# Mamba layer: four engines in the written order, steps of the prologue and epilogue three or four states apart, additions to the sum five states back

## The chip, the cores and the metric

The kernel runs on one core of one Trainium2 chip. The metric is the device time of one execution in microseconds (us). The program computes a stack of eight layers on an activation of 8 sequences x 256 tokens x 128 channels in fp32; the change lies in the seventh of them, `l3_attn`, a bidirectional Mamba layer.

## The reference, cut to what matters

```python
def _mamba(x, ...):                       # E = 256 channels, N = 64 states, R = 8, K = 4
    xp, z = jnp.split(x @ W_in.T, 2, axis=-1)
    xc = _silu(depthwise_conv(xp, conv_w) + conv_b)
    dt_lo, Bm, Cm = split(xc @ W_xp.T, (R, N, N))
    dt = softplus(dt_lo @ W_dt.T + dt_b)
    A = -jnp.exp(A_log)                   # E x N
    def step(h, inp):                     # over 256 tokens
        dA = jnp.exp(dtt[:, :, None] * A)
        h = dA * h + (dtt * xt)[:, :, None] * Bt[:, None, :]
        y = jnp.einsum('ben,bn->be', h, Ct)
        return (h, y)
    y = ys + xc * Dp
    return (y * _silu(z)) @ W_out.T

# the layer: x + norm(ref(norm(x))), where ref is
xn = _layernorm(x, ln1_w, ln1_b)
x1 = _mamba(xn, m1...)
x2 = flip(_mamba(flip(xn), m2...))
return _layernorm(x1 + x2, ln2_w, ln2_b) + xn
```

## The kernel before, in words

The sequences go two at a time: four groups g, and in each the forward Mamba (m = 0) and the backward one (m = 1), which makes eight units u of 64 states each, 512 states in all. A state is one of the N = 64 columns of A, and its work for a whole unit is done at once: a tile of 128 channels x (2 sequences x 2 channel halves x 256 tokens), 128x1024 fp32.

One pass i of the main loop handles several states in different phases:

- `start(i)`: SP fetches C of the state over all partitions (`Cs`, five buffers); ACT computes `dA` = exp(dt*A) in two instructions (L2053, three buffers), and for even states four scaled copies `sT` (L2050).
- `inputs(i-1)`: PE writes the input term of the state into PSUM, `ps_h`, by eight transposes of `sT` (L2068, even states) or by 32 small products with `dB` (L2066, odd states). POOL makes `dB` for two odd states at a time (L2040, `pre`). `ps_h` shares three PSUM buffers (tag "b") with every `ps_a` of the prologue and the epilogue.
- `scan(i-1)`: DVE runs the recurrence over all 1024 columns (L2074) into `h` (three buffers). Then h is multiplied with C into `hc` (L2076, four buffers): on POOL, and in every eighth state on DVE, where the scan works in place in PSUM.
- `add(i-4)`: PE adds `hc` to the sum of the unit, `ps_y`, by eight transposes (L2086). There is one buffer of `ps_y`.

Between these lie the steps of two generators, one step a pass: `behind` is the epilogue of the unit that has just ended, and `ahead` is the prologue of the next one, begun in pass n = 6 of a unit. A `yield` ends a step. The prologue normalises x (m = 0 only; `norm_steps` twice, and ln1 on POOL, L1916 and L1917), transposes it (L1924 or L1926, copy L1928), convolves (L1937, L1939), projects (L1944, L1946), applies Silu (L1948), makes B, C and dt (L1953, L1956, L1959 to L1970) and dtx (POOL, L1973; PE L1983, ACT L1985). The epilogue copies `ps_y` (ACT, L1992), transposes it back (PE, L1997), adds D*xc (DVE, L2001, two instructions), multiplies with silu(z) (POOL, L2003) and projects (PE, L2009); after m = 1 it also adds x1 and x2 (DVE, L2022), normalises (`norm_steps`, twice) with three POOL operations between (L2024, L2026, L2028) and one at the end (L2033).

`norm_steps` is DVE statistics (L227, L228), two small POOL operations for the inverse root (L230, L231), a small DVE operation on their result (L234), and four ACT instructions (L237).

The first six layers run under `as_written`, which chains the instructions of PE, DVE, ACT and POOL in the order in which the program issues them. The Mamba layer does not: there the compiler's list scheduler decides the order on each engine from the dependencies, and it moves steps against each other. SP's queue is under the scheduler in both.

Of the kernel before, what the change touches and what calls it, by code (L numbers as in the profile page):

```python
# [8 lines left out]
F32 = mybir.dt.float32  # L9
# [3 lines left out]
ALU = mybir.AluOpType  # L13
# [159 lines left out]
class Ctx:  # L173
# [45 lines left out]

    def norm_steps(self, dst, src, n):  # L220

        nc = self.nc
        st = self.small.tile([P, n, 6], F32, name="ln_st")
        mv = self.small.tile([P, n, 2], F32, name="ln_mv")
        rs = self.small.tile([P, n], F32, name="ln_rs")
        for i in range(n):
            nc.vector.bn_stats(out=st[:, i, :], in_=src[:, i, :])  # L227
            nc.vector.bn_aggr(out=mv[:, i, :], in_=st[:, i, :])  # L228
        yield
        nc.gpsimd.tensor_scalar(rs, mv[:, :, 1], EPS, None, ALU.add)  # L230
        nc.gpsimd.tensor_tensor(rs, rs, self.mhalf.to_broadcast([P, n]), ALU.pow)  # L231
        for i in range(4):
            yield
        nc.vector.scalar_tensor_tensor(mv[:, :, 0], mv[:, :, 0], -1.0, rs, ALU.mult, ALU.mult)  # L234
        yield
        for i in range(n):
            nc.scalar.activation(dst[:, i, :], src[:, i, :], AF.Identity, bias=mv[:, i, 0:1], scale=rs[:, i:i + 1])  # L237
        yield
# [1609 lines left out]
def l3_attn(k):  # L1848
# [17 lines left out]
    with ExitStack() as es:  # L1866
# [10 lines left out]
        for m, w in enumerate(k.l3a):  # L1877


            w["wk"] = s1.tile([P, 4, 256], F32, name="wk", bufs=2)  # L1880
            cv = s2.tile([P, 4, 256], F32, name="cv", tag="sp_u")
            nc.sync.dma_start(out=cv, in_=k.I[f"l3a_m{m + 1}_conv"].partition_broadcast(P))
            nc.vector.tensor_tensor(w["wk"], cv, over(w["win"][:, 0:256], 4, 1), ALU.mult)
            w["A"] = s1.tile([P, 2, N], F32, name="A", bufs=2)
            nc.scalar.activation(w["A"], w["alog"], AF.Exp)
            nc.vector.tensor_scalar(w["A"], w["A"], 1e-20, -1.0, ALU.max, ALU.mult)
        xTs, CLs = [], []
        for j in range(2):
# [20 lines left out]
        def prologue(u, o):  # L1909
            g, m = divmod(u, 2)  # L1910
            w = k.l3a[m]
            if m == 0:
                xs = xns[g] = s2.tile([P, 4, D], F32, name="xn")
                yield from k.norm_steps(xs, k.x[:, 4 * g:4 * g + 4, :], 4)
                yield from k.norm_steps(xs, xs, 4)
                nc.gpsimd.tensor_tensor(xs, xs, over(k.l3a_ln[:, 0, :], 4, 1), ALU.mult)  # L1916
                nc.gpsimd.tensor_tensor(xs, xs, over(k.l3a_ln[:, 1, :], 4, 1), ALU.add)  # L1917
                yield
            xT, CL = xTs[u % 2], CLs[u % 2]
            ps = pb()  # L1920
            for j in range(4):
                d = slice(j * P, (j + 1) * P)
                if m == 0:
                    nc.tensor.transpose(ps[:, 0, d], xns[g][:, j, :], k.ident)  # L1924
                else:
                    nc.tensor.matmul(ps[:, 0, d], xns[g][:, j ^ 1, :], k.flip, start=True, stop=True)  # L1926
            yield
            nc.scalar.copy(xT[:, :, 3:3 + L], by_seq(ps[:, 0, :]))  # L1928
# [4 lines left out]
            for ec in range(2):  # L1933
                for b in range(2):
                    ps = pb()
                    for tap in range(4):
                        nc.tensor.matmul(ps[:, 0, 0:L], w["wk"][:, tap, ec * P:(ec + 1) * P], xT[:, b, tap:tap + L], start=tap == 0, stop=tap == 3)  # L1937
                    yield
                    nc.scalar.activation(xc[:, ec, b * L:(b + 1) * L], ps[:, 0, 0:L], AF.Identity, bias=w["cols"][:, ec, 0:1])  # L1939
                    yield  # L1940
                    yield
            for ec in range(2):
                ps = pb()
                nc.tensor.matmul(ps[:, 0, :], w["win"][:, 256 + ec * P:256 + (ec + 1) * P], xT[:, :, 3:3 + L], start=True, stop=True)  # L1944
                yield
                nc.scalar.copy(sz[:, ec, :], ps[:, 0, :])  # L1946
# [7 lines left out]
            for j in range(4):  # L1954
                for ec in range(2):
                    nc.tensor.matmul(ps[:, 1, j * 64:(j + 1) * 64], xc[:, ec, j * P:(j + 1) * P], w["wxp"][:, ec, 0:64], start=ec == 0, stop=ec == 1)  # L1956
            yield
            B = s2.tile([P, 4, N], F32, name="B")
            nc.scalar.copy(CL[0:72, :], ps[0:72, 0, :])  # L1959
# [8 lines left out]
            dt = s2.tile([P, 2, U], F32, name="dt")  # L1968
            yield
            nc.scalar.activation(dt, ps, AF.Softplus)  # L1970
            yield
# [4 lines left out]
            yield  # L1976
            yield
            dtxT = s2.tile([P, 4, 2, P], F32, name="dtxT")
            ps = pb()
            for j in range(4):  # L1980
                for ec in range(2):
                    n = 2 * j + ec
                    nc.tensor.transpose(ps[:, n // 4, n % 4 * P:(n % 4 + 1) * P], dtx[:, ec, j * P:(j + 1) * P], k.ident)  # L1983
            yield
            nc.scalar.copy(dtxT.rearrange("p (a j) e c -> p a (j e c)", a=2), ps)  # L1985
            o.update(xc=xc, sz=sz, cd=cd, dt=dt, dtxT=dtxT, dtxTt=turned("dtxTt", dtxT), B=B, Bt=Bt)

        def epilogue(u, o):
# [3 lines left out]
            nc.scalar.copy(yT.rearrange("p j e c -> p (j e c)"), o["py"].rearrange("p j e c -> p (j e c)"))  # L1992
            yield
            py = pb()
            for ec in range(2):
                for j in range(4):
                    nc.tensor.transpose(py[:, ec, j * P:(j + 1) * P], yT[:, j, ec, :], k.ident)  # L1997
            yield
            t = s2.tile([P, 2, U], F32, name="t", tag="sp_u")
            for ec in range(2):  # L2000
                nc.vector.scalar_tensor_tensor(t[:, ec, :], o["xc"][:, ec, :], w["cols"][:, ec, 2:3], py[:, ec, :], ALU.mult, ALU.add)  # L2001
            yield
            nc.gpsimd.tensor_tensor(t, o["sz"], t, ALU.mult)  # L2003
            yield
            yield
            ps = pb()
            for j in range(4):
                for ec in range(2):
                    nc.tensor.matmul(ps[:, 0, j * D:(j + 1) * D], t[:, ec, j * P:(j + 1) * P], w["wout"][:, ec, :], start=ec == 0, stop=ec == 1)  # L2009
            xs = s2.tile([P, 4, D], F32, name=f"x1{m}")  # L2010
            yield
            nc.scalar.copy(xs.rearrange("p i d -> p (i d)"), ps[:, 0, :])
# [5 lines left out]
            for j in range(4):  # L2018
                nc.tensor.matmul(ps[:, 0, j * D:(j + 1) * D], k.flip, xs[:, j ^ 1, :], start=True, stop=True)
            yield  # L2020
            xs = x1s[g]
            nc.vector.tensor_tensor(xs, ps[:, 0, :].rearrange("p (i d) -> p i d", d=D), xs, ALU.add)  # L2022
            yield from k.norm_steps(xs, xs, 4)
            nc.gpsimd.tensor_tensor(xs, xs, over(k.l3a_ln[:, 2, :], 4, 1), ALU.mult)  # L2024
# [3 lines left out]
            nc.gpsimd.tensor_tensor(xs, xs, xns[g], ALU.add)  # L2028
            yield
            yn = s2.tile([P, 4, D], F32, name="yn")  # L2030
            yield from k.norm_steps(yn, xs, 4)
            to = k.x[:, 4 * g:4 * g + 4, :]
# [37 lines left out]
        def scan(st, n):  # L2070
            flat = "p b e t -> p (b e t)"
            on_v = n % ON_V == ON_V - 1
            h = st["in"] if on_v else s3.tile([P, 2, 2, L], F32, name="h")
            nc.vector.tensor_tensor_scan(h.rearrange(flat), st["dA"].rearrange(flat), st["in"].rearrange(flat), 0.0, ALU.mult, ALU.add)  # L2074
            st["hc"] = s1.tile([P, 2, 2, L], F32, name="hc", bufs=4)
            (nc.vector if on_v else nc.gpsimd).tensor_tensor(st["hc"], h, over(by_seq(st["C"]), 2, 2), ALU.mult)  # L2076

        def add(o, st, n):

            if n == 0:  # L2080
                o["py"] = psumy.tile([P, 4, 2, P], F32, name="ps_y")
            for b in range(2):
                for j in range(2):
                    for ec in range(2):
                        first = n == 0 and j == ec == 0
                        nc.tensor.matmul(  # L2086
                            o["py"][:, 2 * b + j, ec, :], st["hc"][:, b, ec, j * P:(j + 1) * P], k.ident,
                            start=first, stop=n == N - 1, is_transpose=True, skip_group_check=True,
                        )
# [7 lines left out]
        for n in range(3):  # L2097
            pre(made[0], n)
        for i in range(units * N + 4):
            u, n = divmod(i, N)  # L2100
# [12 lines left out]
            if 1 <= i <= units * N:  # L2113
                scan(sts[i - 1], c)
            if i >= 4:
                v, c = divmod(i - 4, N)
                add(made[v], sts.pop(i - 4), c)
                if c == N - 1:
# [56 lines left out]
def program(tc, I, out, layers):  # L2175
    nc = tc.nc
    with ExitStack() as es:
# [39 lines left out]
        for layer in (l3_attn, l3_ffn):  # L2217
            if layer in layers:
                layer(k)
        held[-1].__exit__(None, None, None)  # L2220
# [19 lines left out]
```

## Time and profile before

| | us |
|---|---|
| median of 3 runs | 4112.87 (4107.72 to 4126.58) |
| profiled execution, its own time | 4108.04 |
| its span, first to last instruction | 4106.3 |
| Mamba loop, first scan to last `hc` (2671 to 4023) | 1352 |
| in it: DVE busy / POOL busy / ACT busy / PE busy | 1229.4 / 1239.7 / 1192.5 / 1186.6 |
| granted TensorE clock in the loop | 0.98 |

In the rows of the profile a group of instructions stands with its line, engine, operation, tiles, count, busy time, mean duration in ns, and behind the bar the idle time of the engine just before it with what ended it. "Idle before" in the rows of a timeline stands in square brackets with the releaser. Busy time of two consecutive instructions can overlap a little, so the distance from start to start is used where it is known.

### The profile page before, as it was taken

The page shows a single profiled execution, that of the slowest core. Times are in us where ns is not written, and L with a number is a line of the kernel's source. Part 1 is how long each engine was busy: PE and PEld are TensorE (multiplying, and loading weights), DVE is VectorE, ACT ScalarE, POOL GpSimd, SP SyncE. Part 2 cuts the span into 40 slices and gives each one's busy share as a digit, 9 for nine tenths or more (in the row PEclk, how much of TensorE's full clock was granted, in tenths as well). Part 3 has the DMA queues.
Part 4 walks back from the last instruction along what each step waited for, and adds up shares of the span by engine and source line. Part 5 has one row for each costly group of instructions (what it writes and reads, how often), then busy time and mean ns, then how long its engine had stood idle before and what let it go on. Part 6 is the DMA issues. An engine that isn't in the chain of part 4 may idle for free. (4 is left out here: it accounts for less than half of the span.)

```text
span 4106.3 us, 125005 instructions
## 1 busy us (share of the span) xinstructions
PE 3556.8 (87%) x55183; PEld 2808.9 (68%) x55183; DVE 3015.5 (73%) x4210; ACT 2541.2 (62%) x4481; POOL 2651.4 (65%) x1991
## 2 busy tenths in 40 slices
PE   6899898988898888899998977698988988898886
PEld 4777787777777656565565554387777876877774
DVE  7667768767666666654477677289979988998995
ACT  4445455544445545565454443399979988898893
POOL 5666857856665554522133344389989988998993
PEclk8999999999999999999999998799999999999997
DMA  2000000000001000000000000033323333333430
GB/s 58 3 3 2 3 3 2 3 3 8 3 23 34 1 1 12 20 6 21 1 1 1 6 1 1 26 105 112 110 81 116 111 100 93 111 112 91 115 114 26
DMA packets 98677, 168.89 MB, mean 41 GB/s; under 512 B 16699, under 2 KB 26582, under 8 KB 98006
## 3 DMA queue, kind: packets, MB, share of 16 engines
q1 hardware_dynamic: 98134, 160.89, 13.2%
q8 instruction: 433, 7.09, 0.7%
q14 instruction: 110, 0.90, 0.1%
HBM read 153.51 MB, written 2.10 MB: 38 GB/s over the span
## 5 line engine op out<-in xcount | busy, mean ns | idle before, releaser
L2076 POOL TENSOR_TENSOR hc<-h,Cs 128x1024 f32<-128x1024 f32 x448 | 1050.1, 2373 | 97.8 <-DVE h L2074 85.8
L2074 DVE TENSOR_TENSOR_SCAN h<-dA,ps_h 128x1024 f32<-128x1024 f32 x448 | 989.1, 2267 | 88.9 <-PE ps_h L2068 54.0
L2053 ACT ACTIVATE dA<-dt,A 128x512 f32<-128x512 f32 x1024 | 684.4, 715 | 125.1 <-DVE h L2074 92.2
L2086 PE MATMUL ps_y<-w_c_ident,hc 128*128 128x128 f32 x4096 | 560.9, 281 | 116.1 <-POOL hc L2076 84.1
L2086 PEld LDWEIGHTS ps_y<-w_c_ident,hc 128*128 128x128 f32 x4096 | 453.0, 143 | 171.4 <-POOL hc L2076 156.0
L2050 ACT ACTIVATE sT<-dtxT,B 128x256 f32<-128x256 f32 x1024 | 449.8, 495 | 5.7 <-PE ps_h L2068 5.7
L590 DVE SCALAR_TENSOR_TENSOR acc<-ps,w_l0a_conv,acc 128x254 f32<-128x254 f32 (+2 forms) x768 | 310.3, 472 | 46.9 <-ACT acc L584 46.7
L2066 PE MATMUL ps_h<-dB,dtxTt 64*64 64x64 f32 x16384 | 301.8, 223 | 19.3 <-DVE h L2074 10.1
L2066 PEld LDWEIGHTS ps_h<-dB,dtxTt 64*64 64x64 f32 x16384 | 266.2, 136 | 72.9 <-issue 46.4
L2068 PE MATMUL ps_h<-w_c_ident,sT 128*128 128x128 f32 x2048 | 277.3, 280 | 19.5 <-DVE h L2074 16.9
L2068 PEld LDWEIGHTS ps_h<-w_c_ident,sT 128*128 128x128 f32 x2048 | 240.2, 145 | 31.6 <-DVE h L2074 23.9
L742 POOL TENSOR_TENSOR Ps<-M,w_c_levels 128x512 f32<-128x512 f32 x192 | 241.3, 1274 | 7.2 <-DVE M L716 6.2
L230 POOL TENSOR_SCALAR ln_rs<-ln_mv 128x4 f32<-128x4 f32 (+1 forms) x84 | 22.0, 263 | 336.8 <-DVE ln_mv L228 307.0
L359 ACT COPY XY<-ps 128x1024 f32<-128x1024 f32 (+1 forms) x116 | 108.6, 947 | 152.8 <-PE ps L807 140.5
L800 PE MATMUL ps<-Z,XY 64*64 64x64 f32 x4608 | 169.5, 224 | 21.8 <-DVE Z L784 14.5
L807 PE MATMUL ps<-XY,Z 64*64 64x64 f32 x5120 | 168.8, 222 | 3.5 <-issue 3.5
L800 PEld LDWEIGHTS ps<-Z,XY 64*64 64x64 f32 x4608 | 142.1, 135 | 42.2 <-DVE Z L784 19.3
L1633 ACT ACTIVATE e<-ps,nm 128x256 f32<-128x256 f32 x256 | 99.9, 481 | 96.8 <-DVE nm L1630 69.5
L781 PE MATMUL ps<-XY,Ps 64*64 64x64 f32 x5120 | 115.9, 226 | 48.4 <-issue 11.7
L2074 DVE TENSOR_TENSOR_SCAN ps_h<-dA,ps_h 128x1024 f32<-128x1024 f32 x64 | 145.6, 2275 | 14.9 <-PE ps_h L2066 14.6
L784 DVE TENSOR_TENSOR Z<-ps,w_c_ident 128x512 f32<-128x512 f32 x160 | 107.8, 686 | 60.1 <-PE ps L781 58.6
L807 PEld LDWEIGHTS ps<-XY,Z 64*64 64x64 f32 x5120 | 148.6, 136 | 4.2 <-issue 4.2
(452 smaller groups left out, 8559.8 us busy)
## 6 DMA issues: line engine op xcount, KB each, us to landing
Cs<-cd SPq DMA_DIRECT2D x512, 256.0 KB, 3.3
dtxTt<-dtxT SPq DMA_DIRECT2D x32, 128.0 KB, 4.0
wk<-in_l0a_w SPq DMA_DIRECT2D x8, 256.0 KB, 6.8
w_h<-in_l1f_h SPq DMA_DIRECT2D x4, 512.0 KB, 6.0
w_l2a<-in_l2a_w SPq DMA_DIRECT2D x3, 512.0 KB, 3.8
w_l0a_wg<-in_l0a_wg SPq DMA_DIRECT2D x1, 1024.0 KB
w_qk<-in_l0f_wqkv SPq DMA_DIRECT2D x2, 512.0 KB, 5.3
cv<-in_l3a_m_conv SPq DMA_DIRECT2D x2, 512.0 KB, 4.9
```

What stands on the lines that cost most here:

```text
L590: nc.vector.scalar_tensor_tensor(acc[:, n, s:L], p4[:, n, 0:L - s], conv[:, h2, 4 * j + n, 3 - s:4 - s], acc[:, n, s:L], ALU.mult, ALU.add,)
L742: nc.gpsimd.tensor_tensor(t, M[:, :, 0:64], over(k.l0a_levels[:, n, :], 8, 1), ALU.mult)
L781: nc.tensor.matmul(ps[to, a, at(j)], Ps[own, h, :], XY[own, t, at(i)], start=True, stop=True)
L800: nc.tensor.matmul(ps[own, a, at(j)], XY[rows, t, at(i)], Z[rows, za, at(zj)], start=True, stop=True)
L807: nc.tensor.matmul(ps[to, a, at(4 + j)], Z[rows, za, at(zj)], XY[rows, t, at(i)], start=True, stop=True)
L2050: nc.scalar.mul(st["s"][:, j], o["dtxT"][:, j], o["B"][:, j, n:n + 1])
L2053: nc.scalar.activation(dA[:, :, ec, :], by_seq(o["dt"][:, ec, :]), AF.Exp, scale=w["A"][:, ec, n:n + 1])
L2066: nc.tensor.matmul(ps[q, b, ec, j * 64:(j + 1) * 64], o["dtxTt"][rows, j, ec, q], dB[rows, j, :], start=True, stop=True)
L2068: nc.tensor.transpose(ps[:, j // 2, ec, j % 2 * P:(j % 2 + 1) * P], st["s"][:, j, ec, :], k.ident)
L2074: nc.vector.tensor_tensor_scan(h.rearrange(flat), st["dA"].rearrange(flat), st["in"].rearrange(flat), 0.0, ALU.mult, ALU.add)
L2076: (nc.vector if on_v else nc.gpsimd).tensor_tensor(st["hc"], h, over(by_seq(st["C"]), 2, 2), ALU.mult)
L2086: nc.tensor.matmul(o["py"][:, 2 * b + j, ec, :], st["hc"][:, b, ec, j * P:(j + 1) * P], k.ident, start=first, stop=n == N - 1, is_transpos ...
```

## The change

The Mamba layer now runs under `as_written` on PE, DVE, ACT and POOL. Its generators get more `yield`s, so that a step on one engine and the step that uses its result lie two to four passes apart where it was one. `add` works five states back rather than four, with five buffers of `hc`. `norm_steps` takes the number of passes before the DVE step and before the ACT step, and has a form in which one pass stands for two normalisations in a row (var*(1+EPS)+EPS*EPS under the root); the prologue's two become one. The D*xc term moves from DVE to PE: eight products of `xc` with a diagonal tile `D` open the sum `ps_y`, and the epilogue's two DVE instructions and its POOL multiplication become one DVE multiplication of `ps_a` with silu(z). Two diagonal tiles are made at the layer's start.

```diff
-    def norm_steps(self, dst, src, n):
+    def norm_steps(self, dst, src, n, twice=False, steps=(4, 1)):
...
-        nc.gpsimd.tensor_scalar(rs, mv[:, :, 1], EPS, None, ALU.add)
+        if twice:
+            nc.gpsimd.tensor_scalar(rs, mv[:, :, 1], 1.0 + EPS, EPS * EPS, ALU.mult, ALU.add)
+        else:
+            nc.gpsimd.tensor_scalar(rs, mv[:, :, 1], EPS, None, ALU.add)
         nc.gpsimd.tensor_tensor(rs, rs, self.mhalf.to_broadcast([P, n]), ALU.pow)
-        for i in range(4):
+        for i in range(steps[0]):
             yield
         nc.vector.scalar_tensor_tensor(mv[:, :, 0], mv[:, :, 0], -1.0, rs, ALU.mult, ALU.mult)
-        yield
+        for i in range(steps[1]):
+            yield
...
+            w["D"] = s1.tile([P, 2, P], F32, name="D", bufs=2)
+            for ec in range(2):
+                nc.vector.tensor_scalar(w["D"][:, ec, :], k.ident, w["cols"][:, ec, 2:3], None, ALU.mult)
...
-                yield from k.norm_steps(xs, k.x[:, 4 * g:4 * g + 4, :], 4)
-                yield from k.norm_steps(xs, xs, 4)
+                yield from k.norm_steps(xs, k.x[:, 4 * g:4 * g + 4, :], 4, True, (3, 3))
...
-                yield
+                for _ in range(4):
+                    yield
...
             yield
+            yield
             nc.scalar.copy(xT[:, :, 3:3 + L], by_seq(ps[:, 0, :]))
...
             t = s2.tile([P, 2, U], F32, name="t", tag="sp_u")
-            for ec in range(2):
-                nc.vector.scalar_tensor_tensor(t[:, ec, :], o["xc"][:, ec, :], w["cols"][:, ec, 2:3], py[:, ec, :], ALU.mult, ALU.add)
-            yield
-            nc.gpsimd.tensor_tensor(t, o["sz"], t, ALU.mult)
+            nc.vector.tensor_tensor(t, py, o["sz"], ALU.mult)
+            yield
...
-            yield from k.norm_steps(xs, xs, 4)
+            yield from k.norm_steps(xs, xs, 4, steps=(3, 3))
...
-            st["hc"] = s1.tile([P, 2, 2, L], F32, name="hc", bufs=4)
+            st["hc"] = s1.tile([P, 2, 2, L], F32, name="hc", bufs=5)
...
             if n == 0:
                 o["py"] = psumy.tile([P, 4, 2, P], F32, name="ps_y")
+                for j in range(4):
+                    for ec in range(2):
+                        nc.tensor.matmul(
+                            o["py"][:, j, ec, :], o["xc"][:, ec, j * P:(j + 1) * P], w["D"][:, ec, :],
+                            start=j % 2 == ec == 0, stop=False, skip_group_check=True,
+                        )
...
-        for i in range(units * N + 4):
+        for i in range(units * N + 5):
...
-            if i >= 4:
-                v, c = divmod(i - 4, N)
-                add(made[v], sts.pop(i - 4), c)
+            if i >= 5:
+                v, c = divmod(i - 5, N)
+                add(made[v], k.l3a[v % 2], sts.pop(i - 5), c)
...
-                layer(k)
+                with as_written(tc, COMPUTE if layer is l3_attn else ()):
+                    layer(k)
```

The same single `yield` is added after the PE step of the convolutions, of both projections, of B and C, of dt, of the transposed dtx, and in the epilogue after L1992, L1997, L2009 and L2019; two more are added after dtx.

## Prediction

> **What bounds the kernel now.** First the stage. The busy times in the Mamba loop (columns: stretch, its length, then busy us and instructions of PE, PE weight load, DVE, ACT and POOL, then the granted clock):
>
> ```profile
> 2671.00:4023.00 1352.00, 1186.64 (x23218) 1046.04 (x23218) 1229.42 (x683) 1192.50 (x2207) 1239.68 (x630) 0.98 0.36 105
> ```
>
> DVE and POOL each work some 91% of it. Neither can shrink much, so what an edit can win is the 1352 - 1229.4 = 122.6 us in which DVE stands still. The groups that make the load:
>
> ```profile
> L2076 POOL TENSOR_TENSOR hc<-h,Cs 128x1024 f32<-128x1024 f32 x448 | 1050.1, 2373 | 97.8 <-DVE h L2074 85.8
> L2074 DVE TENSOR_TENSOR_SCAN h<-dA,ps_h 128x1024 f32<-128x1024 f32 x448 | 989.1, 2267 | 88.9 <-PE ps_h L2068 54.0
> ```
>
> By the timeline seven scans in a row start 15.25 us before the next one (2.18 each), and a state on DVE takes 2.31 + 1.15 = 3.46. Eight states: 7 x 2.18 + 3.46 = 18.72 on DVE. Four `hc` in a row take 9.28 (2.32 each), a `dB` 1.02; POOL's eight are 7 x 2.32 + 2 x 1.02 = 18.28. So POOL gains only 0.44 per eight states: whatever else it gets, DVE soon waits for through the three buffers of `h`. Then DVE's waits in the loop (us, times, longest):
>
> ```profile
> DVE h L2074 <- PE ps_h L2068: 54.0, 17, 35.7
> DVE ln_mv L234 <- POOL ln_rs L231: 30.4, 10, 3.7
> DVE h L2074 <- PE ps_h L2066: 15.9, 15, 3.2
> DVE ps_h L2074 <- PE ps_h L2066: 14.6, 6, 3.4
> DVE ln_st L227 <- POOL x L2028: 13.3, 3, 4.5
> DVE t L2001 <- PE ps_a L1997: 8.3, 7, 1.9
> DVE h L2074 <- POOL hc L2076: 8.2, 9, 1.8
> ```
>
> Without the 35.7 before the first scan, and with four smaller rows (10.3), they make 119.3. The second and fifth rows, 43.7 us, are small normalisation steps that the scheduler put ahead of scans. The timeline shows one such place, third unit:
>
> ```profile
> 3027.78 2.37 POOL L2076 TENSOR_TENSOR hc<-h,Cs 128x1024 f32<-128x1024 f32 x1 [0.77 <-DVE h L2074]
> 3030.42 1.04 POOL L231 TENSOR_TENSOR ln_rs<-ln_rs,mhalf 128x4 f32<-128x4 f32 x1
> 3031.49 0.17 DVE L234 SCALAR_TENSOR_TENSOR ln_mv<-ln_mv,ln_rs 128x4 f32<-128x4 f32 x1 [3.06 <-POOL ln_rs L231]
> ...
> 3038.30 0.29 DVE L227 BATCH_NORM_STATS2 ln_st<-x 128x6 f32<-128x128 f32 x1 [4.44 <-POOL x L2028]
> ...
> 3040.84 1.97 PE L2068 MATMUL ps_h<-w_c_ident,sT 128*128 128x128 f32 x8 [4.93 <-DVE h L2074]
> ```
>
> DVE stands 3 us for a 0.17 us instruction whose input lies behind an `hc`; PE then runs dry and its eight transposes take 1.97 where they take 1.04 elsewhere. The PE rows of the waits come mostly from here (second unit):
>
> ```profile
> 2927.22 1.94 PE L1953 MATMUL ps_a<-xz,w_l3a_m_wxp 128*72 128x512 f32 x4 [0.39 <-ACT xz L1948]
> 2928.99 1.89 PE L1956 MATMUL ps_a<-w_l3a_m_wxp,xz 128*128 128x64 f32 x16
> 2930.82 1.16 PE L2066 MATMUL ps_h<-dB,dtxTt 64*64 64x64 f32 x64
> ...
> 2932.10 2.30 DVE L2074 TENSOR_TENSOR_SCAN ps_h<-dA,ps_h 128x1024 f32<-128x1024 f32 x1 [3.37 <-PE ps_h L2066]
> ```
>
> The B and C projection waits for Silu, holds PE for 3.6, and the next state's input stands behind it.
>
> **The change part by part, against the profiled execution (4108.04; span 4106.3).**
>
> *Normalisation waits.* In the new order L234 stands four passes behind the statistics and the second L227 two behind L2028, each pass a scan of 2.18. POOL is at most some 5.5 behind (2.37 for its own `hc`, up to 2.9 lag), plus 1.25 for L230 and L231: under four passes. The 43.7 goes. What is late next is POOL itself, below.
>
> *DVE's own work in the loop.* Seven pairs of L2001 at 1.41 become one multiplication from PSUM; nearest row L2076 on DVE, 1.22 (upper bound the pair): 7 x 0.19 = -1.3. Double norms: groups 2 and 3 lose 1.3 each, group 1, formerly done before the loop, brings 1.3. Together -2.6.
>
> *POOL's own work.* L2003 goes (7 x 2.37). There remain, outside the eights, in the loop: dtx 7 x 2.45 = 17.2, roots 9 x 1.27 = 11.4, L2024, L2026, L2028 and L2033 for three groups 15.2, L1916 and L1917 for three 7.6: 51.4. From this come off at most 64 x 0.44 = 28 of slack and 22 of DVE's own small work lying beside it. So 1 to 51 of DVE waits. Taken: 28, by places: dtx 15.8 (each 2.45 less 0.4, more where roots stand before it), L1916/L1917 3 x 1.6, the epilogue's four operations and roots 3 x 2.4.
>
> *PE at Silu and dt.* These steps keep one `yield` between Silu and L1953. Silu ends 4.5 after the scan that frees its pass's `dA`; PE 3.5 later; the input 1.1 more: 9.2, where a scan is due at 7.7 (pass 26, after a DVE state: wait 1.5, four times) or 6.5 (pass 38: 2.7, three times): 14.1. The dt product (1.7 before an input) costs 0.85 x 7 = 6. Sum 20; from 0, if the new lag hides it, to 34, as the three `ps_h` rows have now less the 14 that other steps may own.
>
> *PSUM buffers.* The extra yields hold a `ps_a` one pass longer. In the built program 152 of the 512 inputs wait for the scan two back (127 before), and six for the scan just before: passes 6 and 15 of units 2, 4, 6. Each of the six costs 1.04 to 1.16 and some 0.2: 1.25. Pass 12 waits for an ACT copy after a later `dA`: 0.7. In pass 6 of the four odd and three even units the eight transposes L1997 are late by 0.8 or 1.1. Sum 3 x 3.25 + 3 x 1.1 + 4 x 0.8 = 16. The trace has no such place; bounds 0 and 40, if each second `ps_a` pair behaves so.
>
> *D on PE.* 8 products a unit; L2009 has eight of them at 1.95, eight transposes (L2068) 1.04: 8 to 16 us on PE in all. They stand between an input and `add(0)`, wait for the copy L1992, and end 0.3 before the next input is due. On the path: nothing; without that cover up to 8 x 1.9 = 15.
>
> A rule bears on PE. The eight transposes of a state take 1.04 in the timeline, at a granted clock of 0.98; a pair of states needs 2 x 2.18 of DVE and some 3.9 of PE, so PE has room. The Trainium skill, "TensorE: Matmul & The Clock Gate", Part 4, says that transposes do not count as PE activity, that the clock does not rise to full for them, and gives some 275 ns each. By that estimate three groups of eight would hold PE 6.6 a pair and the layer would gain nothing. The row contradicts it.
>
> *Lag five.* `add` then asks for an `hc` one scan older: 2.2 more before POOL's lag stops PE. It is what makes the 28 a cost through `h` alone; SP's `Cs` (five buffers, landing 3.3) still has over 5 us.
>
> *Start.* In DVE's new order both `wk` (1.2 each, behind the fetch of `cv` that lands at about 2628), A and D stand ahead of the statistics of x, which had been done at 2618. Statistics end at 2633.1, roots, ACT and POOL to 2639.2, where L1924 started at 2633.9: +5.3, in spite of the norm saved. ACT loads Exp after four `sT`, +1.3. First scan +6.6, bounds 3 and 9; the wait before the second scan falls from 3.2 to 1.
>
> *Tail.* L2001 and L2003 (1.41 + 2.4) become 1.22: -2.5.
>
> Sum: waits 119.3 become 28 + 20 + 16 + 1 = 65, so -54; -2.6; +6.6; -2.5: -52.7. 4108.0 - 52.7 = 4055. The median stands 4.8 above the profiled execution: 4060.
>
> **Rivals.**
>
> *The waits nearly all go* (15%). If the longer lags let POOL catch up in the eights, the remaining waits are 1 + 20. Then -98 -2.6 + 6.6 - 2.5, so 4012 (4016 by the median). For it: POOL's load after, 1239.7 - 17.9 + 2.5 = 1224, is no more than DVE's 1227. Against: bursts of 2.45 meet a slack of 0.44.
>
> *No gain* (12%): POOL's 51 in full, PE's 34, PSUM's 30: 116 stay, and the start: -3.3 - 2.6 + 6.6 - 2.5, so 4106 (4111). For it: today's waits on POOL may only be shifted, since DVE has waited there anyway. Against: POOL stood still for 97.8 before `hc`, so it is not what is full.
>
> *Slower* (7%): the PSUM buffers become the bound. Some 100 `ps_a` are made in the loop, each held about two passes; if an input has to wait for the scan just before, it costs 1.25. At 42 such inputs the -52.7 is gone; at 100, 125 - 52.7 = +72: 4180. For it: three buffers for everything, each `ps_a` held longer. Against: six such waits in the built program. That an order is in fact not kept is no rival: the instruction lists of the changed program show the scans unbroken and L234 four scans late.
>
> **How the numbers follow.** Forecast 66%, rivals 15, 12 and 7. A measurement of this kernel can tell some 0.5% (20.6 us) from no change. The forecast's own bounds, POOL 28 less 20 or plus 15 and PE and PSUM about 12 either way, give 4030 to 4090; the range reaches halfway into the two neighbours, 4020 to 4098. Faster (under 4092): nearly all of the forecast and the first rival, 80%. Same 12, slower 8.
>
> **What would show it.** The waits of DVE: no row `ln_mv <- POOL ln_rs` and none on L2028 in the loop; a row of scans waiting for `hc` of 15 to 40 us in place of 8.2. The timeline: a gap of 1.5 to 3 at each L1953, 1.25 at passes 6 and 15 of units 2, 4 and 6. First scan at about 2678. Wrong: a DVE idle sum in the loop above 100, or waits on PSUM in every pass of a prologue.

## The result, and the profile after

The changed kernel takes 4075.9 us (median of 4 runs, 4074.5 to 4079.5); the kernel before took 4119.7 beside it. The ratio is 0.9904, with a 95% interval of 0.9879 to 0.9929: faster by about 1%. The profiled execution took 4076.06 with a span of 4074.1, so 32.2 us of span less than before. The forecast was 4060 (4055 for the profiled execution). The sign held; of the 53 us forecast 32 came between the two profiled executions and 44 between the medians. The terms of the sum were less good than the total.

The same stretch of the profile, with the columns of before (stretch, length, busy us and instructions of PE, weight load, DVE, ACT and POOL, then granted clock, DMA share and GB/s):

```profile
2675.00:3991.00 1316.00, 1180.78 (x23338) 1037.85 (x23333) 1238.21 (x667) 1166.77 (x2205) 1224.63 (x625) 1.00 0.37 108
```

The loop, from the first scan to the end of the last state's `hc` (DVE's; in the change POOL's last one ends 0.9 later), went from 1351.8 to 1315.3. DVE's idle time in it went from 122.4 to 77.1, but its busy time rose from 1229.4 to 1238.2: it had been forecast to fall. The two large groups of the page hardly moved, as they must:

```profile
L2094 POOL TENSOR_TENSOR hc<-h,Cs 128x1024 f32<-128x1024 f32 x448 | 1051.4, 2372 | 95.3 <-DVE h L2092 94.8
L2092 DVE TENSOR_TENSOR_SCAN h<-dA,ps_h 128x1024 f32<-128x1024 f32 x448 | 993.4, 2269 | 93.5 <-ACT dA L2071 44.6
```

DVE's waits in the loop (us, times, longest; the first row holds the 41.5 us before the first scan). Scans are now L2092, `hc` L2094, inputs L2084 and L2086:

```profile
DVE h L2092 <- ACT dA L2071: 44.6, 7, 41.5
DVE h L2092 <- PE ps_h L2084: 21.5, 18, 3.1
DVE ps_h L2092 <- PE ps_h L2084: 17.3, 8, 4.3
DVE h L2092 <- PE ps_h L2086: 11.5, 11, 1.3
DVE h L2092 <- POOL hc L2094: 10.2, 11, 1.8
DVE ps_h L2092 <- ACT dA L2071: 4.2, 3, 1.4
DVE h L2092 <- ACT sT L2068: 3.8, 4, 1.8
```

Without the 41.5 they make 71.6, where 65 had been forecast; gaps of under 0.15 us, which these rows leave out, grew from 3.1 to 5.4. No row of a normalisation is left. The largest single waits are the ones forecast behind Silu (second unit; start, duration, engine):

```profile
2930.78 1.94 PE L1963 MATMUL ps_a<-xz,w_l3a_m_wxp 128*72 128x512 f32 x4 [1.74 <-ACT xz L1958]
...
2934.37 1.16 PE L2084 MATMUL ps_h<-dB,dtxTt 64*64 64x64 f32 x64
2935.66 2.30 DVE L2092 TENSOR_TENSOR_SCAN ps_h<-dA,ps_h 128x1024 f32<-128x1024 f32 x1 [4.27 <-PE ps_h L2084]
```

The part that the forecast did not have is in this timeline of the third unit, and shows as work, not as a wait:

```profile
3052.07 9.33 POOL L2094 TENSOR_TENSOR hc<-h,Cs 128x1024 f32<-128x1024 f32 x4
3053.63 0.83 DVE L238 SCALAR_TENSOR_TENSOR ln_mv<-ln_mv,ln_rs 128x4 f32<-128x4 f32 x1
...
3086.52 4.69 POOL L2094 TENSOR_TENSOR hc<-h,Cs 128x1024 f32<-128x1024 f32 x2
...
3089.48 1.75 DVE L238 SCALAR_TENSOR_TENSOR ln_mv<-ln_mv,ln_rs 128x4 f32<-128x4 f32 x1
```

L238 multiplies four numbers per partition and takes 0.16 to 0.17 us in the tail. Here it ends when the `hc` in flight on POOL ends: the first of the four ends near 3052.07 + 9.33/4 = 3054.4 (L238 at 3054.46), the second of the two at 3091.21 (L238 at 3091.23). So do all nine of the loop. The kernel before showed it already: of the ten in its loop eight took 0.16 to 0.17 us and two 1.22 and 1.23, each with POOL's L2033 beside it, of which this is one:

```profile
3050.99 1.27 POOL L2033 TENSOR_TENSOR x<-x,yn 128x512 f32<-128x512 f32 x1
3051.05 1.22 DVE L234 SCALAR_TENSOR_TENSOR ln_mv<-ln_mv,ln_rs 128x4 f32<-128x4 f32 x1 [3.72 <-POOL ln_rs L231]
```

### The profile page after: what moved, and what is told of

Same layout as the page of the kernel before. It is cut to its first block, busy times and chain, and to the rows that moved or that the text cites. A ratio compares the mean times of both kernels' runs of the same rounds, so it can differ in the third digit from the quotient of the medians.

```text
span 4074.1 us, 125426 instructions
## 1 busy us (share of the span) xinstructions
PE 3549.9 (87%) x55311; PEld 2803.4 (69%) x55311; DVE 3023.3 (74%) x4170; ACT 2509.7 (62%) x4465; POOL 2622.1 (64%) x1975
## 3 DMA queue, kind: packets, MB, share of 16 engines
q8 instruction: 436, 7.14, 0.7%
## 4 chain that ended last, share of the span: by engine, by line
PE 42%; POOL 19%; DVE 17%; issue 13%; ACT 7%; DMA 0%; POOLq 0%; ACTq 0%; DVEq 0%; SPq 0%
POOL hc L2094 12%; PE ps L1523 3%; POOL dB L2058 2%; PE ps L583 2%; DVE acc L595 2%; PE ps L786 2%; DVE h L2092 2%; PE ps L805 1%; PE ps L812 1%; PE ps L1379 1%; PE ps L919 1%; PE ps L859 1%; PE ps L894 1%; DVE nm L1635 1%; PE ps L1609 1%
## 5 line engine op out<-in xcount | busy, mean ns | idle before, releaser
L2094 POOL TENSOR_TENSOR hc<-h,Cs 128x1024 f32<-128x1024 f32 x448 | 1051.4, 2372 | 95.3 <-DVE h L2092 94.8
L2092 DVE TENSOR_TENSOR_SCAN h<-dA,ps_h 128x1024 f32<-128x1024 f32 x448 | 993.4, 2269 | 93.5 <-ACT dA L2071 44.6
L2071 ACT ACTIVATE dA<-dt,A 128x512 f32<-128x512 f32 x1024 | 674.0, 712 | 141.8 <-DVE h L2092 139.5
L2109 PE MATMUL ps_y<-w_c_ident,hc 128*128 128x128 f32 x4096 | 549.4, 277 | 67.7 <-POOL hc L2094 64.5
L2068 ACT ACTIVATE sT<-dtxT,B 128x256 f32<-128x256 f32 x1024 | 433.9, 495 | 0.0
L2084 PE MATMUL ps_h<-dB,dtxTt 64*64 64x64 f32 x16384 | 299.5, 222 | 17.0 <-DVE hc L2094 12.9
L2084 PEld LDWEIGHTS ps_h<-dB,dtxTt 64*64 64x64 f32 x16384 | 264.8, 135 | 71.8 <-issue 49.0
L2086 PE MATMUL ps_h<-w_c_ident,sT 128*128 128x128 f32 x2048 | 277.7, 276 | 20.9 <-DVE h L2092 10.5
L2086 PEld LDWEIGHTS ps_h<-w_c_ident,sT 128*128 128x128 f32 x2048 | 229.3, 142 | 46.8 <-ACT sT L2068 22.3
L805 PE MATMUL ps<-Z,XY 64*64 64x64 f32 x4608 | 169.0, 224 | 20.3 <-DVE Z L789 14.9
L2092 DVE TENSOR_TENSOR_SCAN ps_h<-dA,ps_h 128x1024 f32<-128x1024 f32 x64 | 145.5, 2274 | 21.5 <-PE ps_h L2084 17.3
L786 PE MATMUL ps<-XY,Ps 64*64 64x64 f32 x5120 | 117.6, 228 | 48.4 <-ACT XY L364 11.1
```

The costliest lines, as they stand in the source:

```text
L786: nc.tensor.matmul(ps[to, a, at(j)], Ps[own, h, :], XY[own, t, at(i)], start=True, stop=True)
L805: nc.tensor.matmul(ps[own, a, at(j)], XY[rows, t, at(i)], Z[rows, za, at(zj)], start=True, stop=True)
L2068: nc.scalar.mul(st["s"][:, j], o["dtxT"][:, j], o["B"][:, j, n:n + 1])
L2071: nc.scalar.activation(dA[:, :, ec, :], by_seq(o["dt"][:, ec, :]), AF.Exp, scale=w["A"][:, ec, n:n + 1])
L2084: nc.tensor.matmul(ps[q, b, ec, j * 64:(j + 1) * 64], o["dtxTt"][rows, j, ec, q], dB[rows, j, :], start=True, stop=True)
L2086: nc.tensor.transpose(ps[:, j // 2, ec, j % 2 * P:(j % 2 + 1) * P], st["s"][:, j, ec, :], k.ident)
```

## The experiments

The stretch ahead of the layer is the same code in all these kernels, yet the last addition before the layer ended anywhere between 2603 and 2644 us in their profiled executions. So a kernel is read here by three stretches that leave this out: *start*, from the end of that addition (`x<-x,y` on POOL) to the first scan; *loop*; and *tail*, to the span's end. The loop repeats well: the changed kernel and a kernel that differs from it only ahead of the loop have 1315.31 and 1315.29. The start of the seven kernels that share the change's lies between 52.1 and 52.5. The tail, with unchanged code, varied from 82.6 to 85.6. Sums are of unrounded times. Ratios are to the kernel before, run beside them; its median was 4119.7 beside the change and 4103.5 to 4110.9 beside the others, so ratios compare better than times.

| kernel | ratio (95%) | start | loop | tail | sum |
|---|---|---|---|---|---|
| before | 1 | 47.7 | 1351.8 | 83.3 | 1482.8 |
| the change | 0.9904 (0.9879 to 0.9929) | 52.3 | 1315.3 | 83.5 | 1451.1 |
| scheduler's order | 0.9932 (0.9908 to 0.9957) | 38.9 | 1335.1 | 80.8 | 1454.9 |
| written order alone | 1.0119 (1.0092 to 1.0146) | 55.6 | 1392.2 | 87.0 | 1534.7 |
| lag four | 0.9985 (0.9967 to 1.0003) | 52.1 | 1339.2 | 83.6 | 1474.9 |
| one tensor in L238 | 0.9909 (0.9888 to 0.9929) | 52.3 | 1312.0 | 83.6 | 1447.9 |
| old spacing | 1.0048 (1.0024 to 1.0071) | 52.1 | 1367.6 | 86.2 | 1505.9 |
| weights after the norm | 0.9913 (0.9883 to 0.9944) | 45.0 | 1315.3 | 83.5 | 1443.7 |
| passes at B and C | 0.9893 (0.9849 to 0.9937) | 52.4 | 1306.2 | 82.6 | 1441.1 |
| D off PE | 0.9989 (0.9968 to 1.0009) | 52.3 | 1333.7 | 88.4 | 1474.4 |
| lag six | 0.9899 (0.9865 to 0.9933) | 52.5 | 1312.2 | 83.4 | 1448.1 |
| two norms of x | 0.9949 (0.9927 to 0.9971) | 56.4 | 1320.8 | 85.6 | 1462.7 |
| three edits | 0.9876 (0.9851 to 0.9902) | 44.8 | 1300.8 | 85.5 | 1431.0 |
| three edits, lag six | 0.9868 (0.9842 to 0.9893) | 44.8 | 1301.3 | 83.6 | 1429.7 |

**Scheduler's order.**

```diff
-                with as_written(tc, COMPUTE if layer is l3_attn else ()):
+                with as_written(tc, ()):
```

> The changed kernel with only the written order taken back: the scheduler places the Mamba layer's instructions again, all other parts of the change stay. Theory (the gain is the order: normalisation steps no longer stand ahead of scans): most of the 43.7 us of normalisation waits come back, the layer's loop takes 1340 to 1355 us instead of 1315, the time is 4100 to 4120. Rival (the gain is the work dropped and the longer lag, the order only comes along): 4070 to 4085, and the waits on the small normalisation rows stay under 10 us.

Measured: loop 1335.1, time 4074.2. DVE's waits in the loop (the second row with the 30.8 before the first scan):

```profile
DVE h L2092 <- PE ps_h L2084: 50.9, 23, 5.8
DVE h L2092 <- PE ps_h L2086: 50.4, 20, 30.8
DVE ln_mv L238 <- POOL ln_rs L235: 18.0, 6, 3.2
```

In the loop it lies between the theory and its rival. The normalisation waits are back, but with 18.0 and 3.0 on L228 they are half of before's 43.7, with one norm of x less; PE's rows (76.2 without the 30.8) are larger than the change's 50.3, and the loop is 5 us below the theory's range. Over the layer the theory fails, and the time is in the rival's range. The scheduler starts the loop 13.3 us sooner and ends 2.7 sooner, so 16.0 of the order's 19.8 us are given back. The 3.8 that remain are little more than the 3.0 by which the tail varies with unchanged code, and the two ratios' intervals overlap: that the order adds anything over the whole layer is not shown. Of the 31.7 us that the layer won, 27.9 come without the order: 8.8 at the start, 16.7 in the loop, 2.5 in the tail.

**Written order alone.**

```diff
             if layer in layers:
-                layer(k)
+                with as_written(tc, COMPUTE if layer is l3_attn else ()):
+                    layer(k)
```

> The kernel of before with the written order alone: old steps, additions four states back, both normalisations, D on DVE. Theory (order and wider steps are needed together): with one pass between a POOL step and the DVE step that reads it, the waits stay in other places, a DVE step standing up to 3 us at each of some 20 normalisations and at dtx, Silu and dt: 4095 to 4125. Rival (the order alone is the gain, the steps are only there for show): 4075 to 4085. Second rival (the old steps in written order are worse than the scheduler's): above 4140.

Measured: 4154.3, loop 1392.2: the second rival. The waits run from engine to engine (PE, ACT and DVE in turn):

```profile
PE ps_a L2009 <- POOL t L2003: 29.2, 7, 4.5
ACT x L2012 <- PE ps_a L2009: 37.8, 7, 6.2
DVE h L2074 <- ACT sT L2050: 27.4, 5, 7.6
```

POOL's multiplication `t` is late behind its `hc`; PE stands for it up to 4.5 us with inputs queued behind, ACT stands for PE up to 6.2 with `sT` and `dA` behind it, and the scan waits for those.

**Old spacing.** The change with every `yield` outside the normalisations as it was. Thirteen places; at the convolutions the change had moved a pass from behind ACT's step to ahead of it, and one place, not named above, is a pass behind L2028. Two of them:

```diff
             nc.gpsimd.memset(dt...)
             yield
             yield
-            yield
-            yield
...
             ps = pb()
             (transposes of dtx)
-            yield
             yield
             nc.scalar.copy(dtxT...)
```

> The changed kernel with the old spacing of all steps outside the normalisations (PE to ACT one pass apart, as before); written order, lag five, one norm with its steps (3, 3) and D on PE stay. The loop is counted from the first scan to the end of the last hc: 1351.8 us before, 1315.3 after, 1339.2 with lag four, 1392.2 with the written order alone. Theory (in a written order the spacing is what makes the gain, since an ACT step that stands one pass behind its PE step holds the dA and sT queued behind it): a good half of the 77 us between the written order alone and the change comes back, loop 1340 to 1355. Rival (the normalisations' spacing and the lag are enough): loop 1315 to 1325.

Measured: loop 1367.6, 52.3 above the change and 12.6 above the theory's range. PE waits for POOL, and ACT for PE:

```profile
PE ps_a L1931 <- POOL xn L1924: 24.5, 3, 8.2
PE ps_a L1990 <- POOL dtx L1980: 15.5, 7, 2.4
ACT xT L1935 <- PE ps_a L1931: 16.2, 3, 5.4
```

The change has 4.5 in the first place. Of all parts undone singly, spacing costs the most. What it is worth under the scheduler was not tried.

**Lag four.**

```diff
-            st["hc"] = s1.tile([P, 2, 2, L], F32, name="hc", bufs=5)
+            st["hc"] = s1.tile([P, 2, 2, L], F32, name="hc", bufs=4)
-            if i >= 5:
-                v, c = divmod(i - 5, N)
+            if i >= 4:
+                v, c = divmod(i - 4, N)
```

> The changed kernel with the additions to the sum four states back and four buffers of hc, as before; nothing else is undone. Theory (lag five only keeps POOL's bursts off PE): a burst of 2.4 us on POOL then stops PE ahead of an input, some ten to twenty places at about 0.5 to 1 us each: 4080 to 4095. Rival (the lag is the main part of the gain): 4105 or more. Second rival (the lag does nothing, since the scan is paced by the buffers of h either way): 4074 to 4079.

Measured: loop 1339.2, 4093.4: 23.9 us of loop for one state of lag, more than the 5 to 20 of the theory's places, though the time is within its range. POOL's row is as before the edit (11.1 for 10.2); what grew are PE's wait for `hc` (60.5 us in the change, the longest 1.2) and the inputs that PE then writes late:

```profile
PE ps_y L2109 <- POOL hc L2094: 102.7, 118, 3.7
DVE h L2092 <- PE ps_h L2086: 34.2, 24, 4.1
DVE h L2092 <- PE ps_h L2084: 29.9, 22, 2.6
```

**Lag six.** The same lines with 6 for 5.

> The changed kernel with the additions six states back and six buffers of hc. Lag four had cost 23.9 us of loop against lag five. Theory (what a longer lag buys is PE's freedom from POOL's lag; in the loop PE still waits for an hc 108 times, 60.5 us in all): the loop falls again, but by less, 1305 to 1311. Rival (at lag five POOL already answers through the three buffers of h alone): loop 1313 to 1317 and PE's wait for hc moves to another row. Second rival (a later last addition makes the epilogue late, and the tail 2 us longer): over 1318.

Measured: loop 1312.2, between the theory and its rival. PE's wait for `hc` falls from 60.5 to 3.4 us, and in its place PE waits for `dB` (21.5) and for a free buffer (20.9 on L2092). DVE's waits stay, 73.7. Lag five has nearly all of it.

**D off PE.**

```diff
-            nc.vector.tensor_tensor(t, py, o["sz"], ALU.mult)
+            for ec in range(2):
+                nc.vector.scalar_tensor_tensor(t[:, ec, :], o["xc"][:, ec, :], w["cols"][:, ec, 2:3], py[:, ec, :], ALU.mult, ALU.add)
+            yield
+            nc.gpsimd.tensor_tensor(t, o["sz"], t, ALU.mult)
...
-                        nc.tensor.matmul(o["py"][:, j, ec, :], o["xc"][...], w["D"][:, ec, :], ...)
```

> The changed kernel with the product by D taken off PE again: DVE adds xc times D in two instructions and POOL multiplies by sz, as before, with one pass more for POOL's step; the tiles of D are still made. Theory (a 2.4 us POOL step in each unit comes back as a burst, DVE gets 0.2 more): seven times 0.2 and seven times 0.4 to 2 us of waits, loop 1319 to 1331, tail 2.5 longer. Rival (POOL hides it, nothing of the gain comes from D): loop 1315 to 1318. Second rival (the products by D on PE cost more than they save): loop under 1313.

Measured: loop 1333.7, tail 88.4: 18.4 and 4.9 worse, more than the theory. A wait that it had not named:

```profile
3030.97 0.47 ACT L1949 ACTIVATE xz<-ps_a,w_l3a_m_cols 128x256 f32<-128x256 f32 x1 [3.41 <-POOL t L2020]
```

The next prologue's first convolution goes into the `xz` of two units back, whose `sz` POOL still has to read. ACT stands 3.4 us in three units, 10.2 in all, with `dA` behind it. So POOL's multiplication costs, besides its time, the late release of a buffer; how the 18.4 divide between the two stays open.

**Two norms of x.**

```diff
-                yield from k.norm_steps(xs, k.x[:, 4 * g:4 * g + 4, :], 4, True, (3, 3))
+                yield from k.norm_steps(xs, k.x[:, 4 * g:4 * g + 4, :], 4, steps=(3, 3))
+                yield from k.norm_steps(xs, xs, 4, steps=(3, 3))
```

> The changed kernel with x normalised twice again, as before, each time with steps (3, 3); the second takes eight passes more in the first prologue of a group. Theory (the dropped norm is worth DVE's 1.3 and POOL's 1.27 in three places, one of these a burst that is met by h's buffers): loop 1318 to 1324, first scan 4 to 5 us later, the time 4082 to 4087. Rival (the eight passes more push the rest of the prologue into the time when the next unit needs it): loop above 1328. Second rival (nothing on the path): loop 1314 to 1317.

Measured: loop 1320.8, start 4.2 later: as the theory had it (the median, 4090.6, is above its range, the profiled execution, 4085.7, within).

**One tensor in L238.** The same product, for the three norms of the layer, with the reciprocal root as a scalar per partition:

```diff
-        nc.vector.scalar_tensor_tensor(mv[:, :, 0], mv[:, :, 0], -1.0, rs, ALU.mult, ALU.mult)
+        for i in range(n):
+            nc.vector.tensor_scalar(mv[:, i, 0:1], mv[:, i, 0:1], rs[:, i:i + 1], -1.0, ALU.mult, ALU.mult)
```

> The changed kernel with the small normalisation product of the Mamba layer (two tensors from SBUF, 128x4) written as four instructions of one tensor and per-partition scalars each. Theory (the instruction with two tensors from SBUF cannot run while POOL's hc reads SBUF, and takes up to 1.87 us for 0.16 of work): the nine instructions that took 8.9 us in the loop become 36 of some 0.1 us, under 4.5 us in sum and none over 0.4; the time falls by 3 to 7 us, to 4069 to 4073. Rival (what holds it is the order of the two engines, a wait that the record counts as work): the first of each four still ends with the POOL instruction in flight, the sum stays near 9 us or grows, and the time is 4075 to 4080.

Measured: loop 1312.0, 3.3 less; no instruction of the 36 over 0.21 us. The change first, then this kernel (busy us, mean ns of one):

```profile
L238 DVE SCALAR_TENSOR_TENSOR ln_mv<-ln_mv,ln_rs 128x4 f32<-128x4 f32 x9 | 8.9, 985 | 0.0
```

```profile
L240 DVE TENSOR_SCALAR ln_mv<-ln_mv,ln_rs 128x1 f32<-128x1 f32 x36 | 5.0, 201 | 0.0
```

The sum missed its bound of 4.5 by 0.5, since one takes 0.2 and not 0.1. But the stretch to the end of `hc` is gone while order and steps are the same, so it was the second tensor and not a wait. In the scheduler's order the form with two tensors took 0.165 us in all eight places of the loop: there each starts before the next `hc` does. The Trainium skill, "SBUF — State Buffer", section "Who interferes with whom", says that a DVE instruction with two inputs in SBUF contends with a GpSimd instruction that reads SBUF, and that the later one is blocked for the whole of the other. The rows agree. The ratio alone (0.9909) could not have told this edit from none.

**Weights after the norm.** `cv` is still fetched first; the rest goes behind L1924 of the first prologue.

```diff
-            nc.vector.tensor_tensor(w["wk"], cv, over(w["win"][:, 0:256], 4, 1), ALU.mult)
-            ... A and D of both directions ...
+            cvs.append(cv)
...
                 nc.gpsimd.tensor_tensor(xs, xs, over(k.l3a_ln[:, 1, :], 4, 1), ALU.add)
+                if u == 0:
+                    setup()          # the lines taken out above
```

> The changed kernel with wk, A and D of both directions written after the first normalisation of x in the first prologue instead of ahead of it. Theory (in the written order DVE waits 7.1 us for the fetch of cv and then makes wk, A and D before the statistics of x): from the first wk's place on, 48.1 us until the first scan become 39 to 43; the loop stays 1315; the time falls by 6 to 9 us against the change. Rival (the products of wk, which need cv, are late for PE's convolution instead): 45 to 48, under 3 us in all.

Measured: start 45.0 for 52.3 (from the old place of the first `wk`, 4.1 after that addition, 40.8), loop unchanged: the theory. In the change DVE stood 7.14 us for `cv` with the statistics of x queued behind:

```profile
2627.17 1.23 DVE L1888 TENSOR_TENSOR wk<-cv,w_l3a_m_win 128x1024 f32<-128x1024 f32 x1 [7.14 <-DMA cv<-in_l3a_m_conv]
```

**Passes at B and C.**

```diff
             nc.scalar.activation(xz, xz, AF.Silu)
             yield
+            yield
             (B and C, L1963)
+            yield
             (L1966)
```

> The changed kernel with one pass more between Silu and the B and C projection, and one pass between the projection's two halves. Theory (PE stands for Silu with the next input queued behind it, and 3.6 us in one piece are more than PE's lead): the waits of scans at this place, 24.7 us, fall under 10, the loop from 1315.3 to 1298 to 1306. Rival (the lead is lost whenever any 1.8 us of PE work come between inputs): 15 or more of the waits stay, loop 1308 to 1316. Second rival (a ps_a held one pass longer makes inputs wait elsewhere): loop above 1317.

Measured: loop 1306.2, 9.2 less, at the theory's upper bound. The 4.27 and 3.07 at this place are gone (2.02 and 0.83 are left), and what is next is ACT, which loads a table, runs Silu and loads the next table, 4.5 us in one piece, ahead of a `dA`:

```profile
2920.43 2.30 DVE L2094 TENSOR_TENSOR_SCAN ps_h<-dA,ps_h 128x1024 f32<-128x1024 f32 x1 [2.02 <-ACT dA L2073]
```

**Three edits.** One tensor in L238, weights after the norm and the passes at B and C together.

> The changed kernel with three edits together: the small normalisation product from one tensor and scalars, wk, A and D written after the first normalisation, and the two added passes around the B and C projection. Alone they gave 3.3 and 9.2 us of loop and 7.3 us before the first scan. Theory (three places that do not meet): loop 1302 to 1304, 41 us from the first wk's old place to the first scan, 20 us below the change, 4054 to 4058, some 1.4% below the kernel before. Rival (the waits shift among them): loop 1306 to 1312, 10 to 15 us below the change.

Measured: loop 1300.8, start 44.8: 14.5 + 7.5 us less than the change. The places do not meet, as the theory had it; the loop is 1.2 below its range, and the time, 4064.9, above its range, with a tail 1.9 longer whose code is the same. The sum is 20.1 us below the change and 51.7 below before.

**Three edits, lag six.** The same with 6 for 5 in the lag and in `hc`'s buffers.

> The kernel with the three edits together, and the additions six states back with six buffers of hc. Alone, lag six took 3.1 us off the change's loop, while the waits of DVE stayed (71.6 to 73.7 us) and its own work fell by 4.3, 1.3 of it in the small normalisation product, which is already rewritten here. Theory (lag five has taken nearly all that lag can give): loop 1297 to 1301 where the three edits gave 1300.8, no difference in the time that can be told. Rival (with the projection's waits gone, POOL's lag is the next in line): loop 1288 to 1296. Second rival (the two longer delays make a ps_a or the epilogue late): above 1303.

Measured: loop 1301.3, no gain by the sixth state. Both versions are 1.2 to 1.3% below the kernel before. That they beat the change is shown by the profiled layer alone (20.1 and 21.4 us, one execution each); the intervals of the three ratios overlap.

## Why the prediction was right or wrong

*Normalisation waits, 43.7 forecast to go:* they went, and the unbroken row of scans is as the text had it. But what this bought was overstated. The order that removes them costs 13.3 us at the start and 2.7 in the tail against the scheduler with the same edits, and L238 moved from waiting (30.4) to being blocked (8.9 of work for 3.8).

*DVE's own work, -2.6 forecast, +8.8 measured:* this is the step that failed, in sign and by 11.4 us. The t multiplication gave its 1.3 (9.8 to 8.5). L238 added 5.1. The scans added 4.3 (993.4 for 989.1), 1.0 of it because one takes 2269 ns for 2267. Most of the rest is lost overlap: a scan that starts after a gap does not overlap with the one ahead, and of the pairs of scans in a row 334 overlap where 368 did. 49 scans start late for a buffer of `h` (11 in the row above, 38 by less than 0.15 us) where 9 did. The dropped norm gave no DVE time here: 36 pairs of statistics take 16.0 us where 40 took 15.8, because the written order alternates the two instructions and the scheduler interleaved them (0.44 a pair for 0.40; under the scheduler the changed code's 32 pairs take 0.39). Undone, it costs 5.1 of busy time and 5.5 of loop.

*POOL, 28 forecast:* 10.2 as waits, where 15 to 40 had been named as the sign, 1.6 in the 38 short gaps, and some 3 of the scans' lost overlap, which is counted above: about half of what was taken.

*PE at Silu and dt, 20, and PSUM buffers, 16:* PE's rows make 50.3 for these 36. The Silu places were 4.27 and 2.65 to 3.07 (24.7 in all) where 2.7 and 1.5 (14.1) had been taken, PE standing 1.74 for Silu where it had stood 0.39. In the forecast units (2, 4 and 6) scans waited 1.35, 1.18, 1.31 and 1.13 in each, 14.9 in all, but at states 6, 11, 12 and 23, where passes 6, 12 and 15 had been named; at state 6 PE works without a pause from D's products on, so that wait is not a buffer's. D's products make 4.3 (next), and 6.4 lie at small places that were not forecast. Behind none of the seven dt products does a scan wait for PE, for which 6 had been taken.

*D on PE, nothing on the path:* the trace shows otherwise. The products wait for the copy of the last unit's sum, take 2.05 us, and the next input stands behind them (third unit):

```profile
3004.49 2.05 PE L2102 MATMUL ps_y<-D,xz 128*128 128x128 f32 x16 [1.25 <-ACT yT L2007]
...
3007.34 1.16 PE L2084 MATMUL ps_h<-dB,dtxTt 64*64 64x64 f32 x64
3008.67 2.29 DVE L2092 TENSOR_TENSOR_SCAN h<-dA,ps_h 128x1024 f32<-128x1024 f32 x1 [0.61 <-PE ps_h L2084]
```

This scan, of state 5, waits 0.61 in all seven units that have such a copy ahead, 4.3 us; with D off PE it waits in none. Wrong in the other direction was the worth of what D replaces, 1.3 of DVE time, a share of POOL's 28 and 2.5 in the tail: undone, the loop loses 18.4 and the tail 4.9.

*Lag five, without a term in the sum:* 23.9 us when undone. The working knew what it keeps off (PE stopped by POOL's lag) and gave it no price.

*The rule on transposes:* the loop's granted clock is 1.00 after (0.98 before), with eight transposes still in 1.04 us, so the row was right to be followed. One of the transposes of a state has a duration of 275 to 281 ns in the rows of both kernels, near the page's figure; eight in a row take 1.04 us because they overlap, 0.13 us apart. The estimate of 6.6 had gone wrong by multiplying the duration.

*Start, +6.6 forecast, +4.6 measured; tail, -2.5 forecast, +0.2.* The multiplication did bring the sum x1 2.0 us nearer to the loop's end (11.6 for 13.7 after the last `hc`), but the last layer's first Silu came 37.7 us after that `hc` for 37.1. DVE's statistics gave back some 1.2 of it, ahead of the two roots (2.5 for 2.0 and 3.5 for 2.7 us from what they read to the root); the rest stays open.

Together: forecast -54.2 - 2.6 + 6.6 - 2.5 = -52.7; measured -45.3 (idle) + 8.8 + 4.6 + 0.2 = -31.7. The miss of 21 is DVE's own work (11.4), the waits (9, of which 6.6 in the rows and 2.4 in gaps under 0.15 us) and the tail (2.7), less 2 at the start. That the rows came within 6.6 of their 65 is luck in part: POOL's was 18 too high, PE's 14 too low, and 11.2 stand in rows on ACT, which had no term; the 1 left for the second scan did not show.

The rivals: "nearly all waits go" fell, since PE's rows stayed, 50.3 where it had 20. "Slower through the buffers" stayed at 14.9 us in three units. "No gain" is nearest to what a kernel with one part undone shows: lag four or D off PE leave 0.9985 and 0.9989.

The single parts do not add up. Undone one at a time they cost 52.3 (spacing), 23.9 (lag), 19.8 (order), 18.4 (D) and 5.5 us (norm) of loop, 120 together, where the whole won 36.5: each removes a lateness that the others would otherwise pass on. How the scheduler would do with only the lag or only D changed was not tried, so how its 27.9 us divide among the parts stays open.

## What to carry to other kernels

An order written out by hand is only as good as its spacing: an instruction that waits holds everything queued behind it on its engine, and lateness on the slowest helper (POOL here) goes through PE and ACT back to the engine that sets the pace. So price a change of order with its start and tail, where the scheduler's freedom was worth 16.0 us here, and price a lag by undoing it, not by the waits that still show. Idle time that goes may come back as busy time of the same engine: compare both.

## What the runs showed of the hardware

A 0.16 us DVE product of two tensors in SBUF took up to 1.76 us in the loop while POOL multiplied, and 0.2 us each, 0.56 for the four, as four instructions with one tensor and scalars. The form with scalars is not free of it at every size. In the kernel with the weights after the norm, 128x128 products with scalars ran beside POOL's `xn`, and two A products, first beside it and then not, read:

```profile
2629.33 1.49 POOL L1929 TENSOR_TENSOR xn<-xn,w_l3a_ln 128x512 f32<-128x512 f32 x1 [2.08 <-ACT xn L242]
2629.62 1.29 DVE L1896 TENSOR_SCALAR A<-A 128x128 f32<-128x128 f32 x1
2630.83 1.48 DVE L1899 TENSOR_SCALAR D<-w_c_ident,w_l3a_m_cols 128x128 f32<-128x128 f32 x2
2630.90 1.32 POOL L1930 TENSOR_TENSOR xn<-xn,w_l3a_ln 128x512 f32<-128x512 f32 x1
...
2633.36 0.21 DVE L1896 TENSOR_SCALAR A<-A 128x128 f32<-128x128 f32 x1
```

The same section of the Trainium skill names `tensor_scalar` among the operations that can take the shared pair of ports; that a 128x1 product did not slow beside `hc` (0.19 to 0.21 us in all 36 of the loop) is what these runs add. Why the two sizes differ was not tried.
